# Softmax weights of two attention layers turned by VectorE and DMA in place of TensorE, in a four-layer graph network

## Chip, cores and metric

One core of one Trainium2 chip. The metric is the time of one execution on the device in microseconds (us).

## The reference, cut to what matters

64 graphs of 256 nodes with 256 features, fp32, go through four layers, each behind a layer norm and a relu and added to its input. Layers 0 and 3 are the ones that the change touches:

```python
# x (64, 256, 256), adj (64, 256, 256) int32
h = relu(layernorm(x))
# layer 0: attention, 8 heads of 32
scores = where(adj > 0, q @ k.T / sqrt(32), -1e9)
x = x + (softmax(scores, axis=-1) @ v) @ Wo + bo
# layer 1: graph attention, one head, softmax over axis 1     (not changed)
# layer 2: gated graph network, 3 GRU steps                   (not changed)
# layer 3: graph attention, 4 heads of 64
logits = leaky_relu(s_src[:, :, None, :] + s_dst[:, None, :, :], 0.2)
probs = softmax(where(adj[..., None] == 1, logits, -9e15), axis=2)
x = x + einsum('bijh,bjhc->bihc', probs, f)
```

A softmax runs along the free axis, so its tile has queries on the partitions. The product with v (or f) contracts over keys, so it needs keys on the partitions. That is why the weights have to be turned: 12 tiles of 128x1024 for a pair of graphs, 8 in layer 0 and 4 in layer 3.

## The kernel before

The 64 graphs go in 32 pairs. Every operation of every pair is first recorded as a task with a modelled duration; a list scheduler then fixes the order of all instructions on all engines at build time, two pairs interleaved. It tries several settings and keeps the order with the lowest modelled span. The parts that the argument needs (cuts marked with "..."):

```python
key = (round(begin, digits), (t.layer == 2) == (engine == "PE"), t.pair, t.order)   # next task: lowest key
...
# weights: loaded, turned and multiplied ahead of the loop, in a pool of their own
with tc.tile_pool(name="prep", bufs=1) as prep:
    ...
# layer 0, for each graph g and each half ti of its queries
add((PE, 1.11, scores), reads=[qT, kT], writes=banks, claims=[*ss, zs, mx, rz])
for half in range(2):
    s = ss[half]
    for j in range(2):                         # score eviction, 128x512 (L605)
        add((V, dve(N2), lambda ...: nc.vector.scalar_tensor_tensor(...)), reads=[b, mb], writes=[(s, j)])
    ...                                        # max, exp with sums, reciprocal
    for k in range(2):
        ps = bank()
        ...                                    # two rows divided, on ScalarE or VectorE
        def turn(s=s, k=k, ps=ps):             # L641
            for i in range(2):
                for c in range(2):
                    nc.tensor.transpose(tok(ps(), P)[:, 2 * i + c, :],
                                        tok(s(), N)[:, 2 * k + i, c * P : (c + 1) * P], ident)
        add((PE, 4 * TURN, turn), reads=[(s, k)], writes=[ps], claims=[pT[2 * half + k]])
        add(evict(N2, ...pT[2 * half + k]..., ...ps...), ...)   # 128x512, L448 on ScalarE or L449 on VectorE
...
mm(psc()[...], tok(v())[:, 2 * g + c, h * D0 : (h + 1) * D0],
   tok(pT[hh](), N)[:, 2 * cc + c, :], ...)    # L662: moving operand contiguous
...
# layer 3: leaky relu, mask (128x1024), max (L1030), exp, then the same turn (L1042), product L1063
```

## Time and profile before

| | before |
|---|---|
| time, median of 4 runs | 4186.17 us (4184.48 to 4188.14) |
| span of the profiled run, mean granted clock | 4185.2 us, 0.994 |
| TensorE busy | 4111.1 us (98%) |
| VectorE busy | 2971.9 us (71%) |
| TensorE transposes of layers 0 and 3 | 3072 |

In the lines of the profile PE is TensorE, PEld its weight loads, DVE VectorE, ACT ScalarE, POOL GpSimd, and SPq the queue of SyncE, which issues the DMAs; the granted clock is the share of TensorE's full clock that the chip granted. One more reading helps to compare: the middle of the run repeats itself. In the chain that ended last, in order of time (start, length, what), the same piece of layer 2 returns once for every pair:

```profile
2004.03 10.30 PE ps L840 x24
...
2131.46 10.30 PE ps L840 x24
```

So a pair takes 2131.46 - 2004.03 = 127.43 us. The window over that stretch (columns: stretch, its length, busy us with counts of PE, PEld, DVE, ACT and POOL, granted clock, DMA share, GB/s) shows TensorE at 1995.67 of 2000 us, VectorE at 71%, ScalarE at 62%:

```profile
1600.00:3600.00 2000.00, 1995.67 (x9739) 1264.18 (x9739) 1414.38 (x2787) 1245.55 (x3311) 288.47 (x287) 1.00 0.11 36
```

### The profile page before, as it was taken

What the parts mean: (1) busy time and instruction counts of PE and PEld (TensorE: products, weight loads), DVE (VectorE), ACT (ScalarE), POOL (GpSimd) and SP (SyncE); (2) the same over time, 40 slices, a digit from 0 to 9 for tenths busy, and PEclk for the clock granted to TensorE, in tenths of its full rate; (3) what the DMA queues carried; (4) which work ended last, traced back from release to release, by engine and by line L of the source; (5) the groups of instructions that cost most, each with busy time, mean ns of one, the idle gap of its engine ahead of it and who ended that gap; (6) DMA issues with size and microseconds to landing.
All of it is one profiled execution on the core that took longest, in us unless ns stands there. A gap on an engine that the chain in (4) does not pass through costs nothing.

```text
span 4185.2 us, 56064 instructions
## 1 busy us (share of the span) xinstructions
PE 4111.1 (98%) x20144; PEld 2608.5 (62%) x20144; DVE 2971.9 (71%) x5835; ACT 2540.2 (61%) x6803; POOL 597.4 (14%) x596
## 2 busy tenths in 40 slices
PE   7999999999999999999999999999999999999996
PEld 4665666666666666666666666666666666666654
DVE  5975877776777666777666777667776667786655
ACT  4953766565666555766556666556665557665433
POOL 1011111111111111111111111111111111111111
PEclk9999999999999999999999999999999999999998
DMA  3000111011110101110011101011101111010100
GB/s 93 26 26 31 44 39 36 24 44 33 39 44 23 40 29 38 44 40 24 28 44 38 44 27 38 28 39 44 44 21 31 41 38 49 25 34 28 34 31 26
DMA packets 125670, 151.53 MB, mean 36 GB/s; under 512 B 9552, under 2 KB 112848, under 8 KB 125392
## 3 DMA queue, kind: packets, MB, share of 16 engines
q1 hardware_dynamic: 125392, 147.95, 11.1%
q8 instruction: 159, 2.61, 0.3%
q14 instruction: 119, 0.97, 0.1%
HBM read 130.82 MB, written 17.10 MB: 35 GB/s over the span
## 4 chain that ended last, share of the span: by engine, by line
PE 84%; ACT 8%; DVE 7%; issue 1%; DMA 0%; SPq 0%; POOL 0%; POOLq 0%; DVEq 0%; ACTq 0%
PE ps L840 26%; PE ps L920 15%; PE ps L821 8%; PE ps L570 5%; PE ps L532 4%; ACT w L546 3%; PE ps L641 3%; PE ps L1063 3%; PE ps L718 3%; PE ps L1042 3%; PE ps L776 3%; PE ps L509 2%; PE ps L591 2%; ACT w L628 2%; PE ps L662 2%; PE ps L906 1%
## 5 line engine op out<-in xcount | busy, mean ns | idle before, releaser
L546 ACT ACTIVATE w<-w,mx 128x256 f32<-128x256 f32 x1664 | 823.9, 502 | 144.4 <-DVE mx L612 90.6
L448 ACT COPY w<-ps 128x512 f32<-128x512 f32 x1024 | 567.4, 584 | 531.5 <-PE ps L821 217.5
L840 PE MATMUL ps<-w,whhT 128*128 128x512 f32 x1536 | 722.4, 596 | 0.3 <-ACT w L448 0.3
L840 PE MATMUL ps<-w,giT 128*128 128x512 f32 x1536 | 718.1, 594 | 0.0
L840 PEld LDWEIGHTS ps<-w,giT 128*128 128x128 f32 x1536 | 284.9, 190 | 342.4 <-issue 337.9
L449 DVE COPY w<-ps 128x512 f32<-128x512 f32 x448 | 300.1, 684 | 232.9 <-PE ps L906 89.3
L840 PEld LDWEIGHTS ps<-w,whhT 128*128 128x128 f32 x1536 | 278.6, 190 | 252.9 <-issue 242.6
L920 PE MATMUL ps<-giT,w 128*128 128x512 f32 (+1 forms) x1024 | 361.6, 488 | 0.0
L920 PE MATMUL ps<-whhT,w 128*128 128x512 f32 (+1 forms) x1024 | 360.5, 489 | 0.0
L821 PE MATMUL ps<-w,w 128*128 128x256 f32 x1536 | 353.2, 380 | 0.0
L605 DVE SCALAR_TENSOR_TENSOR w<-ps,mask 128x512 f32<-128x512 f32 x512 | 332.4, 675 | 16.7 <-PE ps L591 16.7
L546 ACT ACTIVATION_READ_ACCUMULATOR w<-w,mx 128x1 f32 x1664 | 322.5, 194 | 0.0
L821 PEld LDWEIGHTS ps<-w,w 128*128 128x128 f32 x1536 | 287.0, 190 | 51.7 <-issue 14.9
L612 DVE TENSOR_REDUCE mx<-w 128x4 f32<-128x1024 f32 x256 | 307.8, 1202 | 1.2
L628 ACT ACTIVATE w<-w,rz 128x256 f32<-128x256 f32 x704 | 302.1, 501 | 7.3 <-DVE rz L619 7.0
L920 PEld LDWEIGHTS ps<-giT,w 128*128 128x128 f32 x1024 | 190.9, 190 | 147.7 <-issue 129.6
L641 PEld LDWEIGHTS ps<-ident,w 128*128 128x128 f32 x2048 | 235.8, 140 | 74.2 <-issue 46.7
L877 POOL TENSOR_TENSOR w<-w,w 128x512 f32<-128x512 f32 x128 | 163.6, 1279 | 752.6 <-ACT w L872 752.5
L641 PE MATMUL ps<-ident,w 128*128 128x128 f32 x2048 | 262.6, 273 | 2.3 <-DVE w L605 1.5
L920 PEld LDWEIGHTS ps<-whhT,w 128*128 128x128 f32 x1024 | 188.1, 191 | 99.9 <-issue 85.0
L974 POOL TENSOR_TENSOR w<-w,w 128x512 f32<-128x512 f32 x64 | 82.2, 1284 | 1138.3 <-ACT w L973 1138.3
L1018 ACT ACTIVATE w<-w,f 128x256 f32<-128x256 f32 x512 | 215.4, 499 | 8.7 <-DMA w<-row 8.7
(132 smaller groups left out, 6188.3 us busy)
## 6 DMA issues: line engine op xcount, KB each, us to landing
w<-in_adj_dram SPq DMA_DIRECT2D x128, 512.0 KB
w<-row SPq DMA_DIRECT2D x64, 512.0 KB
x<-in_x_dram SPq DMA_DIRECT2D x64, 256.0 KB
out_dram<-x SPq DMA_DIRECT2D x64, 256.0 KB
w<-row SPq DMA_DIRECT2D x32, 256.0 KB
gg_sb<-in_L_gnn_weight_dram SPq DMA_DIRECT2D x3, 256.0 KB
wih_sb<-in_L_gnn_w_ih_dram SPq DMA_DIRECT2D x1, 768.0 KB
whh_sb<-in_L_gnn_w_hh_dram SPq DMA_DIRECT2D x1, 768.0 KB
```

The lines of the kernel that those rows point to most:

```text
L448: (A, act(n), lambda: nc.scalar.copy(dst(), src())),
L449: (V, dve(n), lambda: nc.vector.tensor_copy(dst(), src())),
L546: nc.scalar.activation(tok(e(), N)[:, i, :], tok(e(), N)[:, i, :], AF.Exp, bias=mx()[:, m : m + 1], accum_out=zs()[:, z : z + 1],)
L570: mm(ps(), w[:, k, o * P : (o + 1) * P], tok(hT(), N2)[:, k, :], start=k == 0, stop=k == 1)
L605: (V, dve(N2), lambda s=s, j=j, b=b, t=t: nc.vector.scalar_tensor_tensor(tok(s(), N)[:, 2 * j : 2 * j + 2, :], tok(b(), N), SCALE, tok(mb( ...
L612: (V, dve(4 * N), lambda s=s, mx=mx, h4=h4: nc.vector.tensor_reduce(mx()[:, h4], tok(s(), N), AX.X, ALU.max, negate=True)),
L628: op(tok(s(), N)[:, i, :], tok(s(), N)[:, i, :], rz()[:, z : z + 1])
L641: nc.tensor.transpose(tok(ps(), P)[:, 2 * i + c, :], tok(s(), N)[:, 2 * k + i, c * P : (c + 1) * P], ident,)
L821: mm(ps()[:, g * N : (g + 1) * N], tok(h())[:, t, o * P : (o + 1) * P], tok(am(), N)[:, t, :], start=c == 0, stop=c == 1,)
L840: mm(ps(), w[:, k, c0 : c0 + P], at_o(src, k), start=n == 0, stop=n == 2 * len(terms) - 1)
L920: mm(out, chunk(src, k, t), w[:, k, c0 : c0 + n], start=m == 0, stop=m == 2 * len(terms) - 1)
L1018: (A, act(N, 1), lambda t=t, g=g, h=h, e=e: nc.scalar.activation(tok(e(), N)[:, h, :].rearrange("p (c n) -> p c n", n=P), sd[g]().rearrang ...
```

## The change

Its intent is to take the 96 transposes a pair off TensorE, which is full, drop the 24 evictions of their results (copies of TensorE's output by ScalarE or VectorE), and give the work to engines and queues that are not full. Four heads' weights lie in one tile by blocks, VectorE turns every 32x32 block in place in one instruction, one DMA writes the tile to DRAM, and four DMAs bring it back with each block on the 32 partitions where it belongs. In layer 0 the keys are taken two by two, so that the product reads its moving operand at every second element. The product that makes v takes its stationary operand at every second token to match (`keys` in the kernel; 216 ns from start to start in the median before and after, so no price of it shows). The score evictions of layer 0 become twice as many at half the width. Besides that, the preparation of the weights becomes tasks in the same order, the small buffers get more copies, and the scheduler's key and choices change.

```diff
-                        key = (round(begin, digits), (t.layer == 2) == (engine == "PE"), t.pair, t.order)
+                        key = (round(begin, digits), (first if engine == "PE" else self.OTHERS)[t.layer], t.rank)
 ...
-        "mx": (8, [P, H0], FP, 2),
+        "mx": (12, [P, H0], FP, 2),
 ...
+        "turn": (8, [P, T * N], FP, 0),          # in DRAM
 ...
-    with tc.tile_pool(name="prep", bufs=1) as prep:
-        ...                                       # all weights ahead of the loop
+    def weights0(): ...                           # and 1, 2, 3: the same work as tasks
 ...
+    def turn(e, eT, n):
+        blocks = lambda: e().rearrange(f"p (r {n}) -> p r c i", c=2, i=32)
+        add((V, dve(T * N), lambda: nc.vector.transpose(blocks(), blocks())), writes=[e])
+        d = buf("turn")
+        add((SP, 0.6, lambda: nc.sync.dma_start(d(), e())), reads=[e], writes=[d], latency=4.6)
+        for b in range(4):
+            add(
+                (SP, 0.55, lambda b=b: nc.sync.dma_start(
+                    eT()[32 * b : 32 * b + 32, :].rearrange("p (a w) -> p a w", a=4),
+                    d()[:, b * N : (b + 1) * N].rearrange("(a j) w -> j a w", a=4))),
+                reads=[d], writes=[(eT, b)], latency=3.8,
+            )
 ...
 # layer 0 (layer 3 likewise, with turn(e, eT[k], "c i"))
-                        def turn(s=s, k=k, ps=ps):
-                            ...                   # four TensorE transposes, and their eviction
+                turn(e, eT, "i c")
 ...
-                                tok(pT[hh](), N)[:, 2 * cc + c, :],
+                                turned_keys(pT[hh](), cc, c, "i c"),
 ...
+        if p == 0:
+            for plan.rank, weights in ((None, weights0), (0.5, weights1), (1.5, weights2), (2.5, weights3)):
+                weights()
 ...
-    order = plan.best([(spare, digits) for spare in range(6, 12) for digits in (1, 2, 3)])
+    order = plan.best([(s, d, f) for s in range(5, 11) for d in (2, 3) for f in ((0, 0, 2, 1), (1, 1, 2, 0), (1, 0, 2, 1))])
```

## The prediction

> **What bounds the kernel now.** I read the page first (busy shares, slices), then the chain that ended last, then the groups by form, then windows and the order of time of TensorE.
>
> ```profile
> PE 4111.1 (98%) x20144; PEld 2608.5 (62%) x20144; DVE 2971.9 (71%) x5835; ACT 2540.2 (61%) x6803; POOL 597.4 (14%) x596
> PE   7999999999999999999999999999999999999996
> ...
> PE 84%; ACT 8%; DVE 7%; issue 1%; DMA 0%; SPq 0%; POOL 0%; POOLq 0%; DVEq 0%; ACTq 0%
> ```
>
> TensorE is busy 98% of the span, fully in every slice but the first and the last, and it makes up 84% of the chain. Nothing else is near. Where its 74 us of idle time (4185.2 - 4111.1) lie, the windows show (columns: stretch, its length, then busy us of PE, PEld, DVE, ACT, POOL, each with its count; granted clock, DMA share, GB/s):
>
> ```profile
> 0.00:52.00 52.00, 25.81 (x112) 19.04 (x112) 13.83 (x48) 7.02 (x13) 1.96 (x8) 0.93 0.46 137
> 52.00:110.00 58.00, 54.61 (x332) 34.30 (x336) 50.10 (x108) 41.81 (x125) 12.74 (x13) 0.95 0.14 46
> 2000.00:2200.00 200.00, 199.70 (x922) 124.68 (x921) 136.44 (x269) 118.08 (x309) 30.34 (x30) 1.00 0.11 36
> 4080.00:4186.00 106.00, 72.75 (x300) 43.81 (x298) 56.33 (x83) 41.59 (x116) 11.64 (x10) 0.85 0.07 25
> ```
>
> Head: 26 us idle before 52 us (the weights' preparation runs alone; TensorE's first work on tokens starts at 52.3 us), 3 us more up to 110. Tail: 33 us. That leaves only 11 us of idle time in the 3,970 us between. So time here is TensorE's work plus a head and a tail, and TensorE work that is taken away is time, as long as nothing else takes its place.
>
> The groups that the change touches:
>
> ```profile
> L641 PE MATMUL ps<-ident,w 128*128 128x128 f32 x2048 | 262.6, 273 | 2.3 <-DVE w L605 1.5 <-ACT w L448 0.8
> L1042 PE MATMUL ps<-ident,w 128*128 128x128 f32 x1024 | 137.3, 278 | 13.8 <-ACT w L546 13.7
> L449 DVE COPY w<-ps 128x512 f32<-128x512 f32 x448 | 300.1, 684 | 232.9 <-PE ps L906 89.3 <-PE ps L641 70.4 <-PE ps L570 28.3
> L605 DVE SCALAR_TENSOR_TENSOR w<-ps,mask 128x512 f32<-128x512 f32 x512 | 332.4, 675 | 16.7 <-PE ps L591 16.7
> L1030 DVE TENSOR_REDUCE mx<-w 128x4 f32<-128x1024 f32 x128 | 153.8, 1201 | 0.4
> L662 PE MATMUL ps<-w,w 128*32 128x256 f32 x2048 | 123.8, 382 | 0.0
> ```
>
> L641 and L1042 are the transposes of layers 0 and 3 that go. One lasts 273 ns, but they are pipelined: in the chain in order of time eight of them take 0.87 us.
>
> ```profile
> 2060.44 0.87 PE ps L641 x8
> ```
>
> **What the Trainium skill says.** "TensorE: Matmul & The Clock Gate", Part 4: PE-mode transpose: its output goes to PSUM, so that a copy must follow, and one takes about 275 ns in a kernel. The trace agrees (273 ns; copies L448/L449 follow), but 0.87/8 = 109 ns is the cost when they queue. "Vector Engine (DVE) Microarchitecture Reference", §3.8: the VectorE transpose turns 32x32 blocks and sustains one element per cycle per lane. No transpose on VectorE is in this trace; another one-source pass over 128x1024, the reduction L1030, takes 1.20 us, so I use that. "DMA: Bandwidth & Descriptors", Two DMAs through the same engine are not ordered: a DMA that reads what another wrote has to wait for its completion. The trace shows that wait: the small row of layer 3 is issued at 4154.68 us and read back from 4156.09, 1.4 us later. "SBUF — State Buffer" (its note on cachelines): 16-byte lines, fp32 strides are free as long as two accesses hit one line. The new products of layer 0 read their moving operand at every second element, which is just two per line; no strided matmul of this sort is in this trace.
>
> **The change part by part.**
>
> *TensorE.* I summed the distances from the start of one TensorE group to the start of the next over the whole span: L641 takes 237.5 us (116 ns each), L1042 121.6 us (119 ns each). Removed: 359 us. The instruction lists of the two kernels confirm that 3072 transposes go and none comes (12,944 operations to 9,872); the weights' products stay, about 25 us. New work: 4111 - 359 = 3752 us.
>
> *VectorE.* Added: 384 transposes of 128x1024 at 1.2 us: +461. The score eviction L605 is halved in width: 1024 at about 0.39 us (a 128x264 eviction at L1001 is busy 50.2/128) for 512 at 0.65: +67. The instruction lists give 96 more divisions on VectorE at 0.38: +36; layer 3's mask addition in 256 pieces of 0.67 for 128 of 1.21: +17; the mask itself +5. Removed: evictions 448 to 197 at 0.67: -168; additions that move to GpSimd, 44 at 0.69: -30. Sum +388: about 3360 us busy.
>
> *ScalarE.* Evictions 1024 to 513 at 0.554: -283; divisions -96 at 0.43: -41. About 2216 us. Less loaded.
>
> *DMA.* 384 times 512 KB out and 512 KB back are 403 MB. Before, 148 MB took 11.1% of 16 engines over 4185 us, which is 318 GB/s while busy; so the new 403 MB take about 1.27 ms, 33% of some 3870 us, with the old traffic 45%. The issuing queue needs about 0.4 us an issue (observed 0.4 to 0.5): 1920 more are 770 us of 3870. Neither is full.
>
> *Latency.* A turn used to take about 2.5 us (0.9 on TensorE, 0.6 eviction, hops). Now: 1.2 transpose, write and receipt about 3 (1.4 for the small row, plus 512 KB at 318 GB/s), four issues 1.6, landing 2 to 3 (the two 512 KB broadcasts issued from 4156.09 have their first consumer at 4159.99): 8 to 9 us. It is paid openly where nothing else is left to do, at the end; elsewhere two pairs are interleaved and layer 2 (L840, L920, L821 and L906: by the same start-to-start sums 2415 us over 32 pairs, 75 us of the 127 a pair takes) lies beside it.
>
> *Head and order.* Inputs no longer wait for the preparation. First token work could start at about 12 us instead of 52, and the 25 us of weights' work fills gaps. I take 14 us of idle time for the head, down from 29.
>
> Sum: 3752 of work + 14 head + 43 tail (33, plus about 10 for the longer turn) + 11 middle as before + new middle waits. For these I choose 50 us: 128 products (two of layer 0 and two of layer 3 per pair) stand at a fixed place in TensorE's order behind a DMA round trip; 0.4 us each on average is a judgement, not a measurement. Total 3870 us.
>
> **The rivals.**
>
> *A: VectorE becomes the bound.* 3360 of 3870 us is 87%, against 71% before; and in layers 0 and 3 the load is uneven, since their reductions, evictions and transposes come together. Against: 3360 is below 3752, and busy time overstates what a queue of VectorE work costs (a 512-column instruction is recorded at 0.68 us, but in the order of time L868 starts at 2005.81 and the next VectorE instruction at 2006.41, 0.60 later). For: a block transpose at half rate (2.4 us) would add 461 us, 3820 busy, and the time would be 4050 to 4150.
>
> *B: The round trip is the new wait.* A tile being turned and its destination are both held some 8 us longer out of 30 working tiles, the queue that issues is served in order, and a late transpose holds up everything behind it. If each of the 128 products waited 3 us, 384 us would be gone and the time would stay at about 4200. For: the order is fixed at build time, and latency it did not foresee becomes waiting. Against: DMA is at 45% and the issuing queue idle most of the time, TensorE's other pair is there to fill, and 768 evictions less free PSUM banks.
>
> *C: The strided products are slower.* L662 takes 119 us start to start; at double cost 3990 us. L1063 reads runs of 32 and should not change.
>
> **Range and chances.** The floor is 3752 + 14 + 40 = 3806: the low end, 3805. The high end, 3985, leaves 115 us more for mild forms of A, B or C. Slower than 4102 (2% under) needs a full A or B: 0.06 in all, of which 0.01 for over 2% slower. Faster by over 2%: 0.94.
>
> **What would show it.** Right: TensorE near 3750 busy at 97% or so of the span; no group of transposes of layer 0 and 3; VectorE 3300 to 3400 busy with 384 transposes near 1.2 us; DMA share 40 to 50%; L662's and L1063's successors unchanged in mean; first token work before 15 us. Wrong: transposes well over 1.2 us, or TensorE waiting for "DMA w<-turn" ahead of the two products by more than 100 us in all, or its idle time put down to VectorE in the slices of layers 0 and 3.

## The result, and the profile after

| | before | after |
|---|---|---|
| time, median of 4 runs | 4186.17 us | 3914.28 us (3914.06 to 3914.52) |
| ratio, 95% interval | | 0.935 (0.9334 to 0.9367) |
| one pair in the steady middle | 127.43 us | 116.72 us |

Ratios here are the mean time of one kernel's runs over that of the other's of the same rounds, so not quite the ratio of the medians that are quoted.

The kernel became 272 us faster. The page of the changed kernel: busy row, the slices of TensorE and VectorE, the DMA queue, and the chain's shares by engine.

```profile
PE 3807.4 (97%) x17072; PEld 2291.7 (59%) x17072; DVE 3303.9 (84%) x6664; ACT 2251.6 (58%) x6212; POOL 662.7 (17%) x640
...
PE   7899999999999999999999999999999999999995
...
DVE  7767898786987888888899888889988889988864
...
q1 hardware_dynamic: 401904, 550.73, 45.4%
...
PE 90%; DVE 5%; ACT 3%; DMA 1%; issue 1%; SPq 0%; POOL 0%; POOLq 0%; DVEq 0%; ACTq 0%
```

TensorE is still the bound: 97% busy, 90% of the chain (84% before). VectorE went from 71% to 84%, and to 8 or 9 tenths in the second half. The chain in order of time now returns every 2102.15 - 1985.43 = 116.72 us:

```profile
1985.43 10.50 PE ps L906 x24
...
2102.15 10.50 PE ps L906 x24
```

The windows of the changed kernel, columns as before:

```profile
0.00:52.00 52.00, 35.43 (x159) 23.59 (x160) 31.95 (x87) 24.16 (x64) 9.98 (x16) 0.84 0.70 208
110.00:150.00 40.00, 28.78 (x186) 19.84 (x184) 36.03 (x81) 27.41 (x82) 2.54 (x4) 0.83 0.62 191
1600.00:3600.00 2000.00, 2000.00 (x9063) 1204.20 (x9062) 1780.86 (x3600) 1184.71 (x3285) 353.60 (x342) 1.00 0.48 147
3806.00:3913.00 107.00, 64.20 (x235) 35.94 (x233) 54.32 (x83) 33.39 (x90) 10.43 (x9) 0.79 0.32 99
```

Read them as three parts. In the middle (1600 to 3600 us) TensorE has no idle time at all, at the full clock, with VectorE at 1780.86/2000 = 89%. At the start 16.6 us are idle up to 52 us (26.2 before), but 11.2 more between 110 and 150, where the kernel before had none. At the end 42.8 us are idle, in both parts at a lower granted clock (0.84, 0.83, 0.79).

The groups of the changed kernel by form (line, engine, operation, out<-in, shapes, count | busy us, mean ns | idle before, releaser):

```profile
L614 DVE STREAM_TRANSPOSE w<-w 128x1024 f32<-128x1024 f32 x384 | 475.0, 1238 | 22.7 <-ACT w L635 14.4 <-ACT w L709 5.9
L692 DVE SCALAR_TENSOR_TENSOR w<-ps,mask 128x256 f32<-128x256 f32 x1024 | 359.2, 410 | 11.1 <-PE ps L679 11.0
...
L728 PE MATMUL ps<-w,w 128*32 128x256 f32 x2048 | 131.4, 391 | 1.7 <-DVE w L692 1.2 <-DMA w<-turn 0.5
L1117 PE MATMUL ps<-w,f 128*64 128x256 f32 x1024 | 128.6, 393 | 24.7 <-DMA w<-turn 24.7
```

L641 and L1042 are gone; L614 is the block transpose, 1238 ns. L728 is the successor of L662: the products of layer 0 waited 0.5 us in all for the DMA that brings their operand. Those of layer 3 (L1117) waited 24.7 us, and the list of waits (engine, line, releaser: us in total, times, longest) says where:

```profile
PE ps L1117 <- DMA w<-turn: 24.7, 3, 22.1
...
PE ps L972 <- DVE w L960: 20.0, 9, 3.2
```

22.1 of them are one single wait, which ends at 3894.53 us, for the first tile of the last pair; the other two (2.1 and 0.6 us) come after it. The other wait that matters, L972 (TensorE transposes in the GRU of layer 2), is on VectorE. (The line left out, L554 on VectorE, 20.7 us, lies mostly at the two ends: 7.2 before the first work and 9.9 in the tail, where the kernel before has a wait of 9.9 too.)

### The profile page after: what moved, and what is told of

Same layout as the page of the kernel before. It is cut to its first block, busy times and chain, and to the rows that moved or that the text cites. A ratio compares the mean times of both kernels' runs of the same rounds, so it can differ in the third digit from the quotient of the medians.

```text
span 3912.3 us, 54475 instructions
## 1 busy us (share of the span) xinstructions
PE 3807.4 (97%) x17072; PEld 2291.7 (59%) x17072; DVE 3303.9 (84%) x6664; ACT 2251.6 (58%) x6212; POOL 662.7 (17%) x640
## 3 DMA queue, kind: packets, MB, share of 16 engines
q1 hardware_dynamic: 401904, 550.73, 45.4%
q14 instruction: 152, 1.25, 0.1%
## 4 chain that ended last, share of the span: by engine, by line
PE 90%; DVE 5%; ACT 3%; DMA 1%; issue 1%; SPq 0%; POOL 0%; POOLq 0%; DVEq 0%; ACTq 0%
PE ps L906 32%; PE ps L986 16%; PE ps L887 8%; PE ps L659 5%; PE ps L581 5%; PE ps L679 3%; PE ps L1072 3%; PE ps L1117 3%; PE ps L554 3%; PE ps L728 3%; PE ps L784 3%; PE ps L842 3%; PE ps L972 2%; ACT w L635 2%; DVE w L692 1%; PE ps L1132 1%
## 5 line engine op out<-in xcount | busy, mean ns | idle before, releaser
L635 ACT ACTIVATE w<-w,mx 128x256 f32<-128x256 f32 x1536 | 759.7, 499 | 202.1 <-DVE mx L628 200.9
L906 PE MATMUL ps<-w,whhT 128*128 128x512 f32 x1536 | 732.1, 603 | 1.6 <-ACT w L336 0.7
L336 ACT COPY w<-ps 128x512 f32<-128x512 f32 (+1 forms) x515 | 293.7, 578 | 397.4 <-PE ps L887 164.0
L614 DVE STREAM_TRANSPOSE w<-w 128x1024 f32<-128x1024 f32 x384 | 475.0, 1238 | 22.7 <-ACT w L635 14.4
L628 DVE TENSOR_REDUCE mx<-w 128x4 f32<-128x1024 f32 x384 | 453.3, 1202 | 1.2
L692 DVE SCALAR_TENSOR_TENSOR w<-ps,mask 128x256 f32<-128x256 f32 x1024 | 359.2, 410 | 11.1 <-PE ps L679 11.0
L635 ACT ACTIVATION_READ_ACCUMULATOR w<-w,mx 128x1 f32 x1536 | 292.1, 190 | 0.0
L709 ACT ACTIVATE w<-w,rz 128x256 f32<-128x256 f32 x608 | 264.8, 499 | 6.1 <-DVE rz L702 6.1
L542 DVE TENSOR_SCALAR w<-x,mv,rs 128x256 f32<-128x256 f32 x384 | 190.1, 545 | 17.9 <-POOL rs L522 17.6
L950 ACT ACTIVATE w<-ps,brz 128x512 f32<-128x512 f32 x128 | 87.7, 685 | 199.1 <-PE ps L906 199.1
```

What stands on the lines that cost most here:

```text
L336: (A, act(n), lambda: nc.scalar.copy(dst(), src())),
L614: add((V, dve(T * N), lambda: nc.vector.transpose(blocks(), blocks())), writes=[e])
L628: (V, dve(T * N), lambda: nc.vector.tensor_reduce(mx()[:, 0:4], rows_of(e()), AX.XY, ALU.max, negate=True)),
L635: nc.scalar.activation(row, row, AF.Exp, bias=mx()[:, r : r + 1], accum_out=zs()[:, z0(r) : z0(r) + 1])
L692: nc.vector.scalar_tensor_tensor(rows_of(e())[:, 2 * ti + cc], b()[:, cc * N : (cc + 1) * N].rearrange("p (b n) -> p b n", b=4), SCALE, to ...
L709: op(row, row, rz()[:, r : r + 1])
```

## The experiments

What had to be told apart. My theory T: TensorE's work sets the time; the turn's new cost lies beside it; what is missing against the prediction (44 us) comes from the beginning and the end and from small terms of TensorE's own. Rivals: A, VectorE at 84% takes part of the gain; B, the DMA round trip does; C, the products with a stride do; D, the gain is not the turn's at all, but that of the weights' preparation or of another order. Medians of the kernel before beside these runs were 4187.26 (the first four), 4187.47 (the next four) and 4186.53 us (the last four), so times can be set side by side to within some 2 us. In the expectations of the first four runs the letters are others: A is the theory T, B there is the head (a part of D), C the round trip. Line numbers are those of the kernel named; in the experiments they are shifted against the changed kernel's.

### One part of the change at a time: prep_only, turn0_only, turn3_only, old_prep

**prep_only** keeps the new preparation and scheduler, but both layers turn by TensorE as before.

```diff
-                turn(e, eT, "i c")        # layer 0, and layer 3 likewise
+                (the kernel before's tiles, evictions and TensorE transposes)
```

> Weights' preparation in the order, both layers turned by TensorE as before. If TensorE's work sets the time (A), this can save only idle time at the head: first token work at about 8 us instead of 52, of which 25 us of weights' work stay, so at most 17 us: 4169 us (0.996 of before). If a large part of the measured 272 us came from the head (B), it is below 4120.

Measured: 4158.83 us, ratio 0.9933 (0.9918 to 0.9948): 28 us less than before. TensorE's idle time in the first 52 us is 11.7 us against 26.2. The 28 us are more than the 17 that I had put as the most: the first 150 us give 17.6 (29.6 us idle before, 12.0 here), and a pair in the middle also takes 0.28 us less. Preparation and order alone are a tenth of the gain; D falls as the main cause.

**turn0_only** has the new turn in layer 0 only, **turn3_only** in layer 3 only.

```diff
 # turn0_only
-                turn(e, eT[k], "c i")     # layer 3
+                (TensorE transposes of layer 3 as in the kernel before)
 # turn3_only
-                turn(e, eT, "i c")        # layer 0
+                (TensorE transposes of layer 0 as in the kernel before)
```

> Layer 0 turned by VectorE and DMA, layer 3 by TensorE. A: 64 of a pair's 96 transposes go, at 109 ns each back to back 7.0 us a pair, 223 us in all: 3945 us, and in the steady part a period of 127.44 - 7.0 = 120.5 us a pair, within 0.5. Rival C (the round trip is a new wait in one of the layers): the steady period stays above 122 us here or above 125 in the other one.

> Layer 3 turned by VectorE and DMA, layer 0 by TensorE. A: 32 of 96 transposes go, 3.5 us a pair, 112 us in all: 4060 us, steady period 123.9 us within 0.5, and the tail some 10 us longer than before because the last layer's turn is paid openly. Rival C: steady period above 125.

Measured: turn0_only 3990.62 us (0.9531), turn3_only 4079.24 us (0.9743). Against prep_only that is 168 us for layer 0 and 80 for layer 3, 248 together; both at once give 4158.83 - 3914.28 = 245. The totals add up, but with the order replanned for each they are not read that closely (other_order below). The periods of the steady middle tell the same without head and tail:

| turned by VectorE and DMA | us a pair | saved | removed on TensorE, by the prediction's start-to-start sums |
|---|---|---|---|
| none (prep_only) | 127.15 | | |
| layer 3 | 123.53 | 3.62 | 121.6/32 = 3.80 |
| layer 0 | 120.54 | 6.61 | 237.5/32 = 7.42 |
| both (changed kernel) | 116.72 | 10.43 | 11.22 |

prep_only repeats itself after four pairs, turn0_only after two, turn3_only after three and only in a part of its middle; the figures are the means of one such round, and turn3_only's is good to some 0.5 us. 93% of the work removed comes back as time in the middle, and there the two parts add up (10.23 against 10.43). In the uneven first part they do not: TensorE's idle time between 150 and 1550 us is 0.8 us in prep_only, 4.8 and 5.0 with one layer turned, and 26.8 with both. The totals of these two kernels were missed by some 45 and 20 us (3945 and 4060 expected), on the same side as the prediction: not in the period, but around the steady middle. In turn0_only the first 150 us hold 29.8 us of idle time, against 12.0 in prep_only and 13.2 in turn3_only.

**old_prep** turns both layers in the new way, with the preparation ahead of the loop as in the kernel before.

```diff
-            for plan.rank, weights in ((None, weights0), (0.5, weights1), (1.5, weights2), (2.5, weights3)):
-                weights()
+            (the kernel before's preparation, in its own pool ahead of the loop)
```

> Both layers turned by VectorE and DMA, the weights prepared ahead of everything as before. A: 17 us above the changed kernel's 3914, 3931 us, as the preparation is worth the same here; different orders of the same work may move this by 20 us either way. B: above 3980.

Measured: 3998.86 us (0.9551), 85 us slower than the changed kernel, where I had expected 17 and 28 would be the worth of the preparation by prep_only. This is over the line (3980) that I had set for a large part of the gain coming from the head. The first 250 us of old_prep, columns as before:

```profile
0.00:250.00 250.00, 188.84 (x977) 117.81 (x978) 189.87 (x451) 133.47 (x392) 24.88 (x34) 0.88 0.51 154
```

and of the changed kernel:

```profile
0.00:250.00 250.00, 217.93 (x1068) 138.57 (x1069) 178.44 (x419) 136.30 (x385) 27.95 (x36) 0.94 0.50 152
```

29 us of the 85 lie in that beginning. The rest does not: old_prep never settles into a repeated period with a full TensorE (3822.8 us busy, 172 idle over the whole run). The planner makes another order where the tasks of the preparation are absent, so this run mixes the preparation with an order, and does not give the preparation's worth by itself.

### The order alone: other_order

The same work with another of the planner's choices, the one that its model puts second.

```diff
-    order = plan.best([(s, d, f) for s in range(5, 11) for ...])     # its choice: (5, 3, (1, 0, 2, 1))
+    order = plan.best([(7, 2, (1, 1, 2, 0))])
```

> The changed kernel's work without any change, in another of the orders its planner can choose (its second best). Theory: with VectorE only some 2.5 us a pair short of TensorE, the order decides whether TensorE runs full; another order gives 3930 to 3990 and TensorE waiting on VectorE in the middle, as was seen with the old preparation. Rival (the steady part is given by TensorE's work whatever the order): 3905 to 3925.

Measured: 3954.56 us (0.9447), 40 us slower than the changed kernel with the same work, but for some 30 instructions that the planner gives to ScalarE in place of VectorE (VectorE 6634 against 6664 instructions, 3314 against 3304 us busy); 118.3 us a pair late in the run. Between 1600 and 3600 us TensorE is idle for 20.7 us, most of it in waits for VectorE (8.7 at L972, 3.9 at L554, 3.0 at L842), as expected. So an order of the planner's is worth some tens of us here, about as much as my whole miss. It also shows how far single totals such as old_prep's can be read: not closer than that.

### More work on VectorE: dve_some, dve_all

With the order held fixed, a pass over the whole tile (max of the tile with itself, in place, so the result stays right) follows the block transposes: those of layer 3 in **dve_some** (128 more, 145 us busy, 4.5 a pair), all of them in **dve_all** (384 more, 434 us, 13.6 a pair).

```diff
+        def both():
+            nc.vector.transpose(blocks(), blocks())
+            if n == "c i":                        # dve_some; always in dve_all
+                nc.vector.tensor_tensor(e(), e(), e(), ALU.max)
-        add((V, dve(T * N), lambda: nc.vector.transpose(blocks(), blocks())), writes=[e])
+        add((V, dve(T * N), both), writes=[e])
```

> The order of the changed kernel kept as it is; after each of layer 3's 128 transposes VectorE also replaces the tile by the maximum of it and itself (no change in values), about 1.13 us each, 145 us, 4.5 us a pair. In the steady part VectorE is busy 88.5% of 116.72 us, so 13.4 us a pair are free. Theory (TensorE sets the time, VectorE has room): steady period stays 116.7, time 3915 to 3940. Rival A (VectorE is the bound already): the 145 us come through, 4060.

> The same after all 384 transposes: 434 us, 13.6 us a pair, which is just all that VectorE has free (103.3 + 13.6 = 116.9 of 116.72). Theory: VectorE is now as full as TensorE, in a fixed order that does not fit, so the period goes to 120 to 125 and the time to 4020 to 4180. Rival A: 3914 + 434 = 4350.

Measured: dve_some 3990.51 us (0.9531), dve_all 4347.31 us (1.0382, slower than the kernel before). The steady middle of dve_some:

```profile
1600.00:3600.00 2000.00, 1985.60 (x8946) 1193.41 (x8946) 1841.49 (x3615) 1164.39 (x3222) 349.50 (x337) 1.00 0.46 143
```

and of dve_all, with the shares of its chain from its page:

```profile
1600.00:3600.00 2000.00, 1874.43 (x8081) 1105.87 (x8080) 1807.96 (x3380) 1046.94 (x2891) 321.57 (x310) 0.97 0.42 130
```

```profile
DVE 46%; PE 41%; issue 4%; DMA 3%; ACT 3%; SPq 2%; POOL 0%; DVEq 0%; POOLq 0%; ACTq 0%
```

My expectations failed in both: dve_all came out where rival A put it (4350). I had taken VectorE's idle time, 11% of 116.72 or some 13 us a pair, for room. Of 4.5 us added, about 2.0 showed as time (a pair takes 118.7 us), so some 2.5 were room. In dve_all no room is left to see: 433 us more time for 434 us more work, the chain led by VectorE at a busy share of only 90%, and TensorE, waiting more, at a lower clock (0.97). So rival A is a near miss: in the changed kernel TensorE leads, but by dve_some VectorE is only some 2 us a pair behind in this fixed order. One reservation: the pass added lies between transpose and DMA, so it also makes the turn 1.1 us later. In dve_some TensorE waited little for the DMA all the same (30.3 us in all, 24.4 of them the last wait). In dve_all it did not: the longest of TensorE's waits in total is for the turn of layer 0, 0.5 us in the changed kernel:

```profile
PE ps L734 <- DMA w<-turn: 72.3, 23, 4.7
```

A pair takes some 131 us there, 14.6 more for 13.6 added. So the 433 us are not VectorE's work alone; the later turn (rival B) has a share that these runs do not separate.

### Less work on VectorE: divide_on_act

The opposite: the 416 divisions that the planner gave to VectorE in layer 0 go to ScalarE (58% busy), order fixed.

```diff
-    (V, 2 * 0.33, lambda f=divided, rows=rows: f(nc.vector.tensor_scalar_mul, rows), True),
+    (V, 2 * 0.33, lambda f=divided, rows=rows: f(nc.scalar.mul, rows), True),
```

> The changed kernel in its own order, with layer 0's 416 divisions that VectorE did given to ScalarE (0.34 us each on VectorE, 4.4 us a pair). If VectorE's lateness makes TensorE's waits in the first 1,550 us, these shrink: steady period 116.7 as before, 3885 to 3905. Rival (the waits are the order's own, or ScalarE's longer chain makes new ones): 3914 or above.

Measured: 4037.04 us (0.9642), 123 us slower, where I had expected some 10 to 30 faster. VectorE fell to 79%, and TensorE waits in the middle (1947.87 of 2000 us busy), above all on ScalarE (39.9 of the 52 us idle there; the line is that of the whole run):

```profile
PE ps L1132 <- ACT w L336: 53.2, 25, 2.5
```

So a lighter VectorE gave nothing in this order. The instructions moved stand in an order made for another split, and TensorE waits for ScalarE's evictions. This doesn't say what a new order for this split would give; it says that a busy share is not read as a bound without the order.

### The round trip: back_twice, tail_only

**back_twice** was to make the way back twice as heavy: each of the four DMAs is issued twice onto the same place.

```diff
+                for again in range(2):
-                nc.sync.dma_start(eT()[32 * b : 32 * b + 32, :]..., d()[:, b * N : (b + 1) * N]...)
+                    nc.sync.dma_start(eT()[32 * b : 32 * b + 32, :]..., d()[:, b * N : (b + 1) * N]...)
```

> The order kept; each of the four DMAs back is issued twice, the second over the first, so that a turn's round trip is some 3 us longer, the issuing queue has 1536 issues more (600 us) and the DMA share rises from 45 to about 60%. Theory: the round trip is hidden in the steady part: period 116.7, time 3920 to 3950 (the tail and the uneven start pay). Rival B (TensorE waits for the round trip): 128 products wait 3 us more each, up to 384 us, period 120 to 128.

Measured: 7261.63 us (1.7337). The experiment was flawed: the second DMA writes what the first writes, so it has to wait for it, and that wait stands in the one queue that issues everything. The waits of that queue:

```profile
SPq L621 <- DMA w<-turn: 3520.5, 1536, 4.6
```

1536 waits of 2.29 us are 3520 us, and the time grew by 3347. It does not test whether the trip as it is lies hidden; for that there is only the trace of the changed kernel (one wait of 0.5 us for it in the first 150 us, then none before the tail), and dve_all, where a turn 1.1 us later, on a fuller VectorE, brought waits for it in the middle. It shows by accident what would undo the change: a wait in the issuing queue for each of the DMAs back.

**tail_only** takes the round trip away where the trace shows it open: layer 3 of the last pair is turned by TensorE, all else as in the changed kernel.

```diff
+            dma = p < B // 2 - 1          # layer 3 by VectorE and DMA in all pairs but the last
```

> The changed kernel in its own order; only layer 3 of the last pair is turned by TensorE again, as nothing else is left for TensorE there. If the last turn's round trip is paid openly (some 8 us against 2.5), the time falls by 6 to 12 us, to 3902 to 3908. If the tail is bounded by something else, it stays at 3914.

Measured: 3902.94 us (0.9323), 11.3 us less, as expected. The last wait halves, and is now on the softmax itself:

```profile
PE ps L1221 <- ACT w L595: 13.1, 2, 11.2
```

The wait of 22.1 us was for the first tile of that pair. What the round trip consists of, for the last of its four tiles in the changed kernel. The last block transpose, from the timeline of VectorE (start, length, engine, line, what):

```profile
3893.80 1.25 DVE L614 STREAM_TRANSPOSE w<-w 128x1024 f32<-128x1024 f32 x1 [1.05 <-ACT w L635]
```

What follows it, from the chain in order of time:

```profile
3894.89 0.43 SPq L619
...
3895.42 4.15 DMA turn<-w
...
3899.66 0.30 SPq L619
...
3900.95 3.71 DMA w<-turn
...
3904.79 1.72 PE ps L1117 x8
```

From the start of the transpose to the product are 3904.79 - 3893.80 = 11.0 us: 1.25 on VectorE, 0.37 until the queue has issued an earlier tile's DMA back (L619) and takes the write, 4.15 for the write, some 1.4 for the receipt and the issue of four DMAs, 3.71 for the last of them. I had put 8 to 9 us.

### The stride: runs_of_32

The products of layer 0 read runs of 32 in place of every second element. The result is wrong (relative error 0.41).

```diff
-                                turned_keys(pT[hh](), cc, c, "i c"),
+                                turned_keys(pT[hh](), cc, c, "c i"),
```

> Wrong result on purpose: layer 0's product reads its moving operand in runs of 32 elements instead of every second one, everything else and the order kept. If the stride costs (C), its matmuls go back from 60.9 to 57.6 ns start to start in the steady part, 0.2 us a pair, and the time falls by about 7 us to 3907; if the 60.9 was only waits, both stay.

Measured: 3908.84 us (0.9334), 5.4 us less; a pair takes 116.55 us in place of 116.72, and the group, to be read against L728 above:

```profile
L728 PE MATMUL ps<-w,w 128*32 128x256 f32 x2048 | 125.7, 382 | 1.6 <-DVE w L692 1.4 <-DMA w<-turn 0.3
```

From start to start in the middle a product takes 58.3 ns in place of 60.9. The stride has a price, and it is small: C falls.

### A version that beats both: both_ends

TensorE turns where nothing else is there to hide the round trip: both layers of the first pair, and layer 3 of the last; the planner's setting was picked anew for it.

```diff
+            dma = p > 0                   # layer 0
+        dma = 0 < p < B // 2 - 1          # layer 3
-    OTHERS = (1, 1, 0, 2)
+    OTHERS = (2, 1, 0, 3)
+    order = plan.best([(7, 3, (1, 1, 2, 0))])
```

> An attempt at a better version: TensorE turns for the first pair and for layer 3 of the last, where it is not yet or no longer full, VectorE and DMA for the rest; the order chosen anew by the planner out of a wider set. Head idle 20 to about 12 us, tail 8 us shorter, and the planner expects the uneven start to be shorter: 3870 to 3895. If the order is worse in the middle than the planner thinks, up to 3930.

Measured: 3900.35 us (0.9316, 0.9302 to 0.933), the fastest of all, 14 us below the changed kernel and 5 above the range that I expected. Its beginning and its middle:

```profile
110.00:150.00 40.00, 38.94 (x236) 26.18 (x229) 38.57 (x94) 30.37 (x88) 3.38 (x4) 1.00 0.55 181
...
1600.00:3600.00 2000.00, 1991.03 (x8948) 1195.32 (x8950) 1755.67 (x3478) 1175.98 (x3285) 361.00 (x340) 1.00 0.47 146
```

The hole of the changed kernel between 110 and 150 us is closed: idle time in the first 150 us is 16.5 us in place of 31.3. The tail is tail_only's. But this order's middle takes 118.35 us a pair in place of 116.72, which gives part of it back. Against tail_only alone (3902.94) the difference is 2.6 us with overlapping runs, so whether the first pair's share pays is not shown.

## Why the prediction was right, point by point

Predicted 3870 us, measured 3914: the direction, the bound and the range were right, the middle value 44 us (1.1%) too low. In the profile TensorE's busy time is 55 us above the 3752 of the sum, its idle time 13 below the 118.

- **TensorE's work removed is time.** Right: an emptied TensorE was refilled at once, and the steady middle has no idle time. The term was mis-sized: the steady period fell by 127.43 - 116.72 = 10.71 us, 343 us over 32 pairs in place of 359. The sums from start to start had counted waits as work: with each instruction taken from its start to its end, or to the start of the next if that comes first, the transposes removed were busy 348 us, so 11 of the 55 are waits. About 26 more are the clock, by an estimate from the same trace (busy time times (1 - granted clock), instruction by instruction, is 34.5 us after and 8.8 before on the groups that stay). The products of layer 0 are 8 more, some 5 of them the stride (runs_of_32). Some 10 us of the 55 I could not locate.
- **Head.** The step "14 us of idle time for the head, down from 29" failed, and the runs with one part each point to layer 0's turn. The first token work on TensorE did come early, at 7.2 us (predicted: before 15), but the first 150 us hold 31.3 us of idle time, no less than the 29.6 before: the holes moved behind the first scores. The same stretch has 12.0 us in prep_only, 13.2 in turn3_only and 29.8 in turn0_only, so the new preparation did save what I had put, and turning layer 0 by VectorE and DMA gave it back (the planner ordered each of these kernels anew). TensorE ran at the granted clock 0.69 from 25 to 52 us. both_ends, which turns the first pair on TensorE (in another order), has 16.5 us idle there.
- **Tail.** Right: 42.8 us idle in the last 107 against 43 predicted, and tail_only gives the longer turn as 11.3 us against "about 10". That it came out right was in part luck: this trip took 11.0 us rather than 8 to 9, and the prediction's own numbers, 8 to 9 less 2.5 for the old turn, give about 6 and not the "about 10" of its sum.
- **Middle waits on the round trip, 50 us.** Wrong in place and kind: before the tail there is 0.5 us of waits for the DMA. The idle time of the middle (26.8 us between 150 and 1550 us, none from 1600 to 3600, 4.7 from there to 3806) has five waits over 2.5 us, 15.0 us together, all on VectorE (at L972 and L842). So rival B did not happen here; dve_all shows that it is not far off. That the idle time came out only 13 us below the 118 is luck: 17 too little at the head against some 30 too much in the middle.
- **VectorE.** 3304 us busy against 3360; the transposes were 1238 ns against 1.2 us, and the block transpose is not at half rate. The score evictions were the term too high: 359.2 - 332.4 = 27 us more in place of 67. But the reading "3360 is below 3752", that there is room, was too easy: dve_some puts the room at about 2.5 us a pair, dve_all at none.
- **DMA.** 45.4% against 45%. **ScalarE.** 2252 against 2216 us. **Stride.** 391 ns against 382, 5.4 us in all; "unchanged in mean" is nearly right.

How a wait of 2.83 us costs more than itself shows at 867.72 us in the changed kernel, where TensorE waited for VectorE (L832). The windows around it; the clock is the third column from the right:

```profile
866.00:868.00 2.00, 0.28 (x1) 0.30 (x2) 2.00 (x4) 2.00 (x8) 1.10 (x2) 1.00 0.69 242
868.00:870.00 2.00, 2.00 (x7) 1.61 (x6) 2.00 (x6) 2.00 (x6) 1.04 (x1) 0.56 0.01 2
870.00:872.00 2.00, 2.00 (x9) 1.69 (x8) 1.25 (x3) 1.91 (x5) 1.45 (x2) 0.59 0.00 0
872.00:874.00 2.00, 2.00 (x14) 1.77 (x13) 1.82 (x3) 2.00 (x6) 0.45 (x1) 1.00 0.01 4
```

For 4 us after the wait the clock is 0.56 to 0.59 and TensorE does 16 matmuls, where the next 2 us alone have 14 (not all of one size). In the busy row these 4 us look like any others. The windows show the same after a wait of 2.00 us that ends at 1273.91 us (0.61 and 0.54 from 1274 to 1278), but not after one of 3.04 us that ends at 1027.15 (1.00 from 1026 to 1030), so the length of the wait alone does not say it.

What stays open: the 10 us of busy time not located; what the preparation is worth together with the turn (28 us without it, 85 with another order mixed in); and how much longer the round trip could be in the middle without a loss.

## What to carry to other kernels

Work taken off a full engine comes back nearly one for one (here 93% in the steady middle) when what takes its place lies beside it; judge it by the period of one repeated piece in the chain, from start to start, and count the beginning and the end apart, where there is nothing beside it and the old way may be the better one. The busy share of an engine that takes the work over is not its room: add a known dose of work to it and see how much of it shows (and place it where it does not lengthen the path too; mine did). Where a build-time scheduler fixes the order, a single total moves by tens of us with the order alone, so compare periods, or hold the order fixed.

## What the Trainium skill lacked or had wrong

- "Perfetto Trace Analysis", Identifying the Most-Contended Engine, says that for Vector occupancy is also a fair measure of how close one is to roofline. In the steady middle VectorE's occupancy was 89%, 13 us free of 116.72 a pair, and of 4.5 us a pair added about 2.0 became time; at 90% in dve_all 433 of 434 us did. In this fixed order the room was much smaller than the occupancy says (with the reservation that the work added also delayed the turn).
- "DMA: Bandwidth & Descriptors", Issuing engines are not separate DMA queues, says that initiating from several engines saves only the time to initiate. It lacks that a wait in the queue of the issuing engine holds up all that stands behind it: 1536 waits of 2.29 us each made back_twice 3347 us longer.
- "TensorE: Matmul & The Clock Gate", Part 4: PE-mode transpose, gives about 275 ns for one. For 3072 that would be 845 us; they took 116 to 119 ns each from start to start, and taking them away saved 343 us. The figure to budget with is missing. Part 1 of the same page puts the fall of the clock at an idle window of about 3.4 us; here waits of 2.83 and 2.00 us were followed by 4 us at 0.54 to 0.61, and one of 3.04 us was not.
- "Vector Engine (DVE) Microarchitecture Reference", §3.8, gives a rate of one element per cycle per lane, and the trace fits it (1238 ns, beside 1202 ns for the reduction L628 over a tile of the same size); it has no duration for fp32 on a large tile. Measured: 1238 ns for 128x1024 in 32x32 blocks, in place.
- "SBUF — State Buffer", the note on cachelines, has a stride of two fp32 as free. As the moving operand of a product it cost 60.9 in place of 58.3 ns from start to start, 5.4 us in the whole kernel.
